# The end of a transformer block on one core: lane sums by products with ones, another order of projections, and transposes by halves

## The chip, the cores and the metric

The kernel runs on one core of one Trainium2 chip. The metric is the device time of one execution in microseconds (us); smaller is better. A core has five engines with queues of their own that run side by side and wait for one another by semaphores: TensorE (PE in the profile, PEld for its weight loads), VectorE (DVE), ScalarE (ACT), GpSimd (POOL) and SyncE (SP, which issues the DMAs here). SBUF is the memory on the core, PSUM the memory that TensorE writes its products to.

## The reference

The input x is 128 tokens of 512 features. All arithmetic is float32, apart from rounding to 8-bit floats at marked places. Three sublayers are added to x in turn:

```python
x = x + xattn(norm(x), ctx_2048, ...)   # attention to itself and to 12544 context tokens
x = x + attn(norm(x), ...)              # 16 heads of 32, causal
x = x + ffn(norm(x), ...)               # 32 experts, 8 chosen for each token
```

The first projects the tokens to 16 heads of 128 (8 groups of keys and values), attends once to the 128 tokens and once to the context, joins both results to 4096 features, divides by a scale per feature, rounds to 8-bit floats and projects back to 512. The attention to the context is `softmax(q k^T / sqrt(128)) v` with keys and values that are themselves products of the context with a weight. The second sublayer is a plain attention:

```python
Q, K, V = Xn @ Wq + bq, Xn @ Wk + bk, Xn @ Wv + bv
scores = where(causal, Q K^T / sqrt(32), -inf)
return (softmax(scores) V) @ Wo + bo
```

The third normalises, chooses 8 of 32 experts by a softmax over 32 logits, and sums `(silu(x w1) * (x v1)) w2` of the chosen ones with their weights; the kernel computes all experts and multiplies those not chosen by zero.

## The kernel before

Work is written in the order of the code, and a scheduling layer puts it into the queues of the engines; where the code says `tc.issue_after(end)`, an instruction is kept behind `end` in that order. Pools of tiles with a given number of buffers decide what must wait for what: a tile that takes over a buffer waits until the last reader of its former tile is done.

**Preamble** (lines 409 to 622): projections of the tokens, the attention of the tokens to themselves and its part of the projection back. Its first step is `norm_rows` (line 169), which normalises the rows of a 128x512 tile: statistics on VectorE (L173, L174), the variance plus epsilon on GpSimd (L179 or L181), the power -0.5 on GpSimd (L183), and the result on VectorE (L184).

**The chunk loop** (lines 798 to 825) goes over 25 chunks of the context, 512 tokens each but for one of 256. Per chunk it makes keys and values by a seven-product scheme (L329, L348), scores per group transposed, tokens on partitions (L647), a running maximum, the exponential (L729), sums over tokens (GpSimd, L739, into `ol[g][:, 1, :]`, one partial sum per partition, "lane") and the products with the values (L747, added into `ol[g][:, 0, :]` at L752). `ol[g]` is scaled on GpSimd when the maximum grows (L731).

**The end of the attention to the context** (lines 863 to 920). The last chunk's outputs of groups 0 to 7 are made in order. Between them stand the lane sums and the end of the softmax:

- `lane_sums(g, ...)` (line 757) adds the 128 lanes of a group: for each of its two heads a product with the 128 tokens' partial sums as the stationary operand and one column of ones as the moving one (L767), so that the sum of a token lands on the token's partition. For groups 6 and 7 two tiles of exponentials that GpSimd hasn't added yet are further terms. After each second group a reciprocal of 128x4 (L772) goes to `rlat`.
- `finished(b)` (line 775), for block b of two groups: four transposes of a column of `rlat`, broadcast to 128 columns, spread the reciprocals along the free dimension of every partition in PSUM (L781), and VectorE multiplies the outputs by them and by the reciprocal scale (L786).
- `round_block(b)` calls `rounded` (line 198), which rounds to 8-bit floats in six VectorE instructions: two at L203, then L209, L211, L213 and L214, whose result is `cq`.
- `proj(b, cq)` (L857): four products of 128x512 that add to `psx`. It then lets SyncE load the next weight.
- `spin` (line 873): n products of 240 columns that nobody reads, which keep TensorE at work; each stands behind the instruction given.

A float32 product is two instructions in the profile, each with a weight load.

**The second sublayer** (lines 948 to 1064). The mask is put into the scores' PSUM tile as a product with the identity (L956). `norm_rows` and four transposes into one PSUM tile (`transposed`, line 218, L222) give x^T, whose four parts VectorE scales (L966). Then come the queries (`project_T`, 16 products at L978, bias on ScalarE at L984), the values (four products of 512 at L991, bias on VectorE at L996), the keys (`project_T`), the scores of 16 heads (L1007, 16 products of 32 rows) and four fillers. For each of four sets of four heads: maximum (L1022), subtraction (L1024), exponential (L1027), four transposes, copy (L1033), and products with the values (L1036), whose last column is the sum of the softmax. Division (L1044, L1045), transposes, two copies (ScalarE L1053, VectorE L1054), the product with Wo (L1059), seven fillers, and x2 (L1064). PSUM tile `rest_ps` holds half of the products with the values; its unread end takes the fillers.

**The third sublayer** (lines 1068 to 1146): `norm_rows`, four transposes, two copies (L1076, L1077), logits (L1080), the choice of experts (L1082 to L1100), and 16 pairs of experts, `up` (L1111) and `down` (L1132). SyncE loads the first four pairs while the second sublayer runs (L942, L943, L946); the weights of the second sublayer are loaded through the same queue (L135), in the order of the list at line 838.

## Time and profile before

| | |
|---|---|
| median of three runs | 2197.46 us (2194.74 to 2199.66) |
| the profiled execution | 2197.58 us |
| its span, first to last instruction | 2195.8 us |
| mean granted TensorE clock | 0.995 |
| TensorE busy | 2158.6 us (98%) |
| VectorE, ScalarE, GpSimd busy | 1298.3, 900.3, 1075.0 us |
| last lane sums of the last chunk to x1 (L767 first, L958) | 1987.86 to 2020.48 us |
| second sublayer, x1 to x2 (end of L958 to end of L1064) | 2020.48 to 2053.61 us |
| third sublayer, to the store of the result (L1146) | 2053.65 to 2192.65 us |

The page of a profile lists the busy time of each engine, the chain of waits that ended last, and groups of instructions by source line. The timeline lists instructions of one engine, merged when equal ones follow each other: start, length, engine, line, output and inputs, how many, and in brackets how long the engine had sat idle and what released it. An engine that is busy all the time needn't be at full speed: the granted clock (PEclk, 1.00 is full) is a column of its own in the answers by stages. `xN` counts instructions, so a float32 product counts twice.

### The profile page before, as it was taken

How to read it: one execution, taken by the hardware profiler on the slowest of the kernel's cores; microseconds unless marked ns; L12 is line 12 of the kernel's file. 1: busy time of each engine (PE TensorE's matmuls, PEld its weight loads, DVE VectorE, ACT ScalarE, POOL GpSimd, SP SyncE). 2: the span in 40 equal slices, each digit the busy share in tenths (PEclk: the TensorE clock that was granted, in tenths of full speed). 3: DMA queues.
4: the chain of work that ended last, by engine and by line, in shares of the span. 5: the costliest groups of instructions: out<-in, count | busy, mean ns of one | idle time of the engine just before them, and what ended most of it. 6: DMA issues, size and time to landing. Idle time of an engine off the chain costs nothing.

```text
span 2195.8 us, 23886 instructions
## 1 busy us (share of the span) xinstructions
PE 2158.6 (98%) x8700; PEld 1539.2 (70%) x8700; DVE 1298.3 (59%) x2410; ACT 900.3 (41%) x1686; POOL 1075.0 (49%) x1165
## 2 busy tenths in 40 slices
PE   7999999999999999999899999999999999999999
PEld 3667767766776777677667776776777677676654
DVE  7565764675566457557675576567556646757311
ACT  2443444454345444434354344345434444541211
POOL 2314644764564466457554574475457447534000
PEclk9999999999999999999999999999999999999999
DMA  8300000000000000000000000000000000007593
GB/s 296 124 26 1 20 20 1 20 20 0 20 20 20 1 20 20 0 10 20 20 20 0 20 20 20 1 19 20 1 20 19 20 1 20 0 1 264 192 284 118
DMA packets 71221, 95.48 MB, mean 43 GB/s; under 512 B 3136, under 2 KB 39488, under 8 KB 71104
## 3 DMA queue, kind: packets, MB, share of 16 engines
q1 hardware_dynamic: 71104, 93.97, 13.0%
q8 instruction: 68, 1.11, 0.2%
q14 instruction: 49, 0.40, 0.1%
HBM read 93.69 MB, written 0.26 MB: 43 GB/s over the span
## 4 chain that ended last, share of the span: by engine, by line
PE 91%; DVE 5%; POOL 2%; ACT 1%; issue 1%; SPq 0%; DMA 0%; POOLq 0%; ACTq 0%; DVEq 0%
PE a_ps L329 15%; PE o_ps L747 15%; PE s_ps L647 14%; PE a_ps L348 14%; PE c_ps L329 7%; PE c_ps L348 7%; PE gu_ps L1111 4%; PE b_ps L348 4%; PE b_ps L329 4%; PE moe_acc L1132 2%; PE ps_p L462 1%; PE ps_proj L857 1%; PE ps_core L612 1%; POOL ol L739 1%; DVE mxr L658 1%
## 5 line engine op out<-in xcount | busy, mean ns | idle before, releaser
L739 POOL TENSOR_TENSOR ol<-ol,s 128x256 f32<-128x256 f32 x764 | 553.1, 732 | 31.2
L652 ACT ACTIVATE s<-s_ps,krs 128x256 f32<-128x256 f32 x784 | 324.0, 471 | 190.5 <-PE s_ps L647 178.4
L384 POOL TENSOR_TENSOR krs<-kve,mhalf 128x16 f32<-128x16 f32 (+1 forms) x50 | 142.9, 2859 | 528.4 <-DVE kve L382 528.4
L731 POOL TENSOR_TENSOR ol<-ol,al 128x512 f32<-128x512 f32 x192 | 243.5, 1280 | 295.0 <-DVE al L708 295.0
L647 PE MATMUL s_ps<-qxT,KT 128*128 128x256 f32 x1568 | 373.2, 381 | 2.8 <-ACT s L652 2.1
L747 PE MATMUL o_ps<-s,V 128*128 128x256 f32 x1568 | 371.0, 379 | 0.3 <-DVE V L318 0.3
L647 PEld LDWEIGHTS s_ps<-qxT,KT 128*128 128x128 f32 x1568 | 295.6, 190 | 104.6 <-issue 68.2
L658 DVE TRANSPOSE_TENSOR_REDUCE mxr<-s 128x32 f32<-128x1024 f32 (+1 forms) x200 | 242.9, 1215 | 188.0 <-ACT s L652 185.0
L747 PEld LDWEIGHTS o_ps<-s,V 128*128 128x128 f32 x1568 | 297.0, 190 | 41.4 <-DVE V L318 1.1
L729 ACT ACTIVATE s<-s 128x1024 f32<-128x1024 f32 (+1 forms) x200 | 208.3, 1042 | 157.0 <-DVE s L725 153.4
L725 DVE TENSOR_TENSOR s<-s,b_ps 128x1024 f32<-128x1024 f32 (+1 forms) x200 | 231.5, 1169 | 0.0
L299 ACT COPY u<-a_ps 128x512 f32<-128x512 f32 (+1 forms) x198 | 114.3, 577 | 241.2 <-PE a_ps L329 196.1
L329 PE MATMUL a_ps<-ctx,wkv 128*128 128x256 f32 (+1 forms) x800 | 186.2, 375 | 0.6 <-POOL ol L731 0.6
L348 PE MATMUL a_ps<-wkv,ctx 128*128 128x512 f32 x392 | 186.2, 597 | 0.0
L752 DVE TENSOR_TENSOR ol<-ol,o_ps 128x256 f32<-128x256 f32 x192 | 80.0, 417 | 175.6 <-PE o_ps L747 164.7
L329 PEld LDWEIGHTS a_ps<-ctx,wkv 128*128 128x128 f32 x800 | 149.9, 190 | 31.0 <-issue 11.9
L365 DVE TRANSPOSE_TENSOR_REDUCE sqr<-sq 128x16 f32<-128x512 f32 (+1 forms) x200 | 128.1, 678 | 59.8 <-ACT sq L363 59.8
L363 ACT ACTIVATE sq<-KT 128x1024 f32<-128x1024 f32 (+1 forms) x100 | 104.1, 1041 | 137.0 <-DVE KT L318 93.1
L318 DVE TENSOR_TENSOR KT<-c_ps,u 128x512 f32<-128x512 f32 (+1 forms) x50 | 34.1, 681 | 146.4 <-PE c_ps L329 146.3
L348 PEld LDWEIGHTS a_ps<-wkv,ctx 128*128 128x128 f32 x392 | 74.9, 191 | 52.8 <-issue 47.3
L329 PE MATMUL a_ps<-mix,wkv 128*128 128x256 f32 (+1 forms) x400 | 98.8, 391 | 10.6 <-ACT u L299 7.1
L329 PE MATMUL c_ps<-ctx,wsum 128*128 128x256 f32 (+1 forms) x400 | 93.7, 377 | 0.0
(217 smaller groups left out, 2773.8 us busy)
## 6 DMA issues: line engine op xcount, KB each, us to landing
ctx<-in_ctxT SPq DMA_DIRECT2D x23, 1024.0 KB, 5.0
gu<-in_w SPq DMA_DIRECT2D x32, 384.0 KB, 4.7
gu<-in_v SPq DMA_DIRECT2D x32, 384.0 KB, 5.4
dn<-in_w SPq DMA_DIRECT2D x16, 768.0 KB, 4.6
w<-in_wprojT SPq DMA_DIRECT2D x8, 1024.0 KB, 5.6
w<-in_wqxT SPq DMA_DIRECT2D x4, 1024.0 KB, 9.6
w<-in_wqT SPq DMA_DIRECT2D x4, 1024.0 KB, 4.9
wkv<-in_wkvT SPq DMA_DIRECT2D x8, 256.0 KB, 7.3
```

Of the source, the lines that this page charges most:

```text
L329: nc.tensor.matmul(ps[:, j * h : (j + 1) * h], lhsT=w[:, k, (2 * u + j) * D : (2 * u + j + 1) * D], rhs=x[:, k, :], start=first and j == k ...
L348: last_mm[0] = nc.tensor.matmul(ps, lhsT=x[:, k, v * P : (v + 1) * P], rhs=w[:, k, H : 2 * H], start=first and k == 0, stop=k == 1, skip_g ...
L365: nc.vector.tensor_reduce(r[:, 2 * j + i, : n // 32], sq[:, i, :n].rearrange("p (b i) -> p b i", i=32), AX.X, ALU.add, apply_transpose=True,)
L384: nc.gpsimd.tensor_tensor(rs[:, :, :nt], ve[:, :, :nt], mhalf.rearrange("p (g t) -> p g t", g=4)[:, :, :nt], ALU.pow,)
L647: end = nc.tensor.matmul(ps[:, t - t0, :], lhsT=KT[:, g, t * P : (t + 1) * P], rhs=qxT[:, 2 * g : 2 * g + 2, :], start=True, stop=True,)
L652: nc.scalar.activation(s[:, t, :], ps[:, t - t0, :], AF.Copy, scale=rs[:, t : t + 1])
L658: nc.vector.tensor_reduce(mxr[g // 4][:, g % 4, :nt, :].rearrange("p t k -> p (t k)"), s[:, :nt, :].rearrange("p t (k i) -> p (t k) i", i=32),
L725: nc.vector.tensor_tensor(s[:, :nt, :], s[:, :nt, :], ps[:, a, None, :].to_broadcast([P, nt, HS]), ALU.subtract,)
L729: nc.scalar.activation(s[:, :nt, :], s[:, :nt, :], AF.Exp, scale=scale)
L731: nc.gpsimd.tensor_tensor(ol[g], ol[g], alb[:, a, None, :].to_broadcast([P, 2, HS]), ALU.mult)
L739: summed[0] = nc.gpsimd.tensor_tensor(ol[g][:, 1, :], first, s[:, t, :], ALU.add).ins
L747: end = nc.tensor.matmul(ps, lhsT=V[:, t, g * D : (g + 1) * D], rhs=s[:, t, :], start=t == 0, stop=t == nt - 1,)
```

## The change

Five edits, all but the first behind the chunk loop's last chunk:

1. `norm_rows`: the variance plus epsilon (L179, L181) moves from GpSimd to VectorE. The function is used three times: in the preamble and at the start of the second and third sublayers.
2. Lane sums: ones (128x128) become the stationary operand and the partial sums (128x256) the moving one, so that each sum lands on all 128 partitions at once. The transposes of `finished` go away; instead VectorE takes the reciprocal of a 128x512 PSUM tile into an SBUF tile `inv`, and L786 reads `inv`. The five fillers between the blocks go away, and `finished` and `round_block` are no longer kept behind products.
3. Order of the second sublayer: queries, keys, half of the values' products, scores, the other half; the fillers behind the scores go away, and Wk is loaded ahead of Wv. The bias of the values goes behind the first subtraction.
4. Fillers: two instead of one after the first transposes of the exponentials, none after the transposes of `av`.
5. Transposes by halves: where x^T (both sublayers) and `av`^T are made, two PSUM tiles take two transposes each (`transposed_halves`).

In the changed build the instructions of the chunk loop and of the experts' loop stand in the same order on every engine. In SyncE's queue the load of Wo stands one place earlier, ahead of the first half of the first expert.

```diff
-            nc.gpsimd.tensor_scalar(v, mv[:, 1:2], 1.0 + EPS, EPS * EPS, ALU.mult, ALU.add)
+            nc.vector.tensor_scalar(v, mv[:, 1:2], 1.0 + EPS, EPS * EPS, ALU.mult, ALU.add)
...
-            nc.gpsimd.tensor_scalar(v, mv[:, 1:2], EPS, None, ALU.add)
+            nc.vector.tensor_scalar(v, mv[:, 1:2], EPS, None, ALU.add)
...
+    def transposed_halves(tiles, src):
+
+        for i, ps in enumerate(tiles):
+            for k in range(2):
+                j = 2 * i + k
+                turned[0] = nc.tensor.transpose(
+                    ps[:, k, :], src[:, j * P : (j + 1) * P], ident
+                ).ins
+        return tiles
...
     def lane_sums(g, last):
...
-            terms = [ol[g][:, 1, x]] + [t[:, x] for t in last]
-            for t, y in enumerate(terms):
-                end = nc.tensor.matmul(
-                    ps[:, i : i + 1], lhsT=y, rhs=ones[:, 0:1], start=t == 0,
...
-        if g % 2:
-            nc.vector.reciprocal(rlat[:, 2 * g - 2 : 2 * g + 2], ps[:, g % 4 * 2 - 2 : g % 4 * 2 + 2])
-        return end.ins
...
+        if g % 2 == 0:
+            lsum[g // 2] = ps_t.tile([P, 2, HS], F32, tag="t", name="l_ps")
+        terms = [ol[g][:, 1, :]] + last
+        for t, y in enumerate(terms):
+            end = nc.tensor.matmul(
+                lsum[g // 2][:, g % 2, :], lhsT=ones, rhs=y, start=t == 0,
+                stop=t == len(terms) - 1,
             )
         return end.ins
+
+    def finished(b):
+
+        r0 = _COLS["smooth"][0] + 16 + 4 * b
+        inv = tmp.tile([P, 2, HS], F32, tag="al", name="inv", bufs=3)
+        nc.vector.reciprocal(inv, lsum[b])
+        for h in range(4):
+            x = slice((h % 2) * S, (h % 2 + 1) * S)
+            o = ol[2 * b + h // 2][:, 0, x]
+            nc.vector.scalar_tensor_tensor(
+                o, o, rcol[:, r0 + h : r0 + h + 1], inv[:, h // 2, x], ALU.mult, ALU.mult
+            )
...
-        stream += [w.rearrange("(k p) o -> p k o", p=P) for w in (aWq, aWv, aWk, aWo)]
+        stream += [w.rearrange("(k p) o -> p k o", p=P) for w in (aWq, aWk, aWv, aWo)]
...
-            end = spin(spare[:, :240], sums_of(5), 4)
+            end = sums_of(5)
+        finished(2)
+        cqs[2] = round_block(2)
         with tc.issue_after(end):
             end = proj(0, cqs[0]).ins
         with tc.issue_after(end):
-            finished(2)
-            cqs[2] = round_block(2)
             sums_of(6)
-            end = spin(spare[:, :240], sums_of(7), 1)
-        with tc.issue_after(end):
-            end = finished(3)
-            cqs[3] = round_block(3)
+            end = sums_of(7)
+        finished(3)
+        cqs[3] = round_block(3)
...
+            qa, end = project_T("bq", lambda j: bqs[:, j : j + 1], 1.0 / math.sqrt(AD))
+            ka, end = project_T("bk", lambda j: col("bk", j), 1.0, end)
...
+            with tc.issue_after(end):
+                end = v_part(range(2))
+            with tc.issue_after(end):
+                for j in range(4):
+                    for a in range(4):
+                        r = slice(a * AD, (a + 1) * AD)
+                        end = nc.tensor.matmul(
+                            sps[:, a, j, :], lhsT=qa[r, j, :], rhs=ka[r, j, :], start=False,
+                            stop=True, skip_group_check=True,
+                        ).ins
+            with tc.issue_after(end):
+                end = v_part(range(2, NK))
...
-            end = spin(unread, end, 4)
...
+                if a == 0:
+                    with tc.issue_after(sub.ins):
+                        nc.vector.tensor_tensor(
+                            va[:, :, :AD], ps_v.rearrange("s (h d) -> s h d", d=AD),
+                            bvo[:, 0, :].rearrange("s (h d) -> s h d", d=AD), ALU.add,
+                        )
...
-                if a in (0, 3):
-                    end = spin(unread, turned[0], 1)
+                end = spin(unread, turned[0], 2 if a == 0 else 1 if a == 3 else 0)
...
-                pt = transposed(pps, av.rearrange("s h d -> s (h d)"))
-            end = spin(unread, turned[0], 1)
+                transposed_halves(pts, av.rearrange("s h d -> s (h d)"))
+            end = turned[0]
             avT = post1.tile([P, 4, S], F32, name="avT")
-            nc.scalar.copy(avT[:, 0:2, :], pt[:, 0:2, :])
-            nc.vector.tensor_copy(avT[:, 2:4, :], pt[:, 2:4, :])
+            nc.scalar.copy(avT[:, 0:2, :], pts[0])
+            nc.vector.tensor_copy(avT[:, 2:4, :], pts[1])
```

More of the change, by code (lines that the diff above doesn't have):

```diff
@@ L627, in block_kernel @@
     ol = [olp.tile([P, 2, HS], F32, name=f"ol{g}") for g in range(G)]
-    rlat = keep.tile([S, NH], F32, name="rlat")
     sp = late.enter_context(tc.tile_pool(name="sp", bufs=8, side="right", reuse_waits="tile"))
@@ L757, in lane_sums @@
     def lane_sums(g, last):
-        if g % 4 == 0:
-            lsum[g // 4] = ps_t.tile([S, 8], F32, tag="t", name="l_ps")
-        ps = lsum[g // 4]
-        for h in range(2):
-            i = g % 4 * 2 + h
-            x = slice(h * S, (h + 1) * S)
-            terms = [ol[g][:, 1, x]] + [t[:, x] for t in last]
-            for t, y in enumerate(terms):
-                end = nc.tensor.matmul(
-                    ps[:, i : i + 1], lhsT=y, rhs=ones[:, 0:1], start=t == 0,
-                    stop=t == len(terms) - 1,
-                )
-        if g % 2:
-            nc.vector.reciprocal(rlat[:, 2 * g - 2 : 2 * g + 2], ps[:, g % 4 * 2 - 2 : g % 4 * 2 + 2])
+        if g % 2 == 0:
[6 more added lines that the diff above has]
+            )
         return end.ins
     def finished(b):
-        ps = ps_so.tile([P, 4, S], F32, tag="s", name="ps_inv")
         r0 = _COLS["smooth"][0] + 16 + 4 * b
+        inv = tmp.tile([P, 2, HS], F32, tag="al", name="inv", bufs=3)
+        nc.vector.reciprocal(inv, lsum[b])
         for h in range(4):
-            end = nc.tensor.transpose(
-                ps[:, h, :], rlat[:, 4 * b + h : 4 * b + h + 1].to_broadcast([S, P]), ident
-            )
-        for h in range(4):
-            o = ol[2 * b + h // 2][:, 0, (h % 2) * S : (h % 2 + 1) * S]
-            nc.vector.scalar_tensor_tensor(
-                o, o, rcol[:, r0 + h : r0 + h + 1], ps[:, h, :], ALU.mult, ALU.mult
-            )
-        return end.ins
+            x = slice((h % 2) * S, (h % 2 + 1) * S)
+            o = ol[2 * b + h // 2][:, 0, x]
+            nc.vector.scalar_tensor_tensor(
+                o, o, rcol[:, r0 + h : r0 + h + 1], inv[:, h // 2, x], ALU.mult, ALU.mult
+            )
     def maxima(c, i):
@@ L869, in sums_of @@
             )
-        spare = pps.tile([P, H], F32, tag="ps", name="spare")
         def spin(ps, after, n):
@@ L892, in block_kernel @@
             sums_of(1)
+        finished(0)
+        cqs[0] = round_block(0)
         outputs(c, 4)
@@ L895, in block_kernel @@
         with tc.issue_after(end):
-            finished(0)
-            cqs[0] = round_block(0)
             sums_of(2)
             end = sums_of(3)
+        finished(1)
+        cqs[1] = round_block(1)
         with tc.issue_after(end):
@@ L903, in block_kernel @@
         with tc.issue_after(end):
-            finished(1)
-            cqs[1] = round_block(1)
             sums_of(4)
-            end = spin(spare[:, :240], sums_of(5), 4)
+            end = sums_of(5)
+        finished(2)
+        cqs[2] = round_block(2)
         with tc.issue_after(end):
@@ L953, in block_kernel @@
             sps = pss.tile([S, 4, 4, S], F32, name="sps")
+            rest_ps = pss.tile([S, H], F32, name="ps_av2")
+            unread = rest_ps[:, H - 240 :]
             with tc.issue_after(end):
@@ L962, in block_kernel @@
             norm_rows(xnn, x1, twice=True)
-            pt = transposed(pps, xnn)
+            pts = [pps.tile([P, 2, S], F32, tag="ps", name="ps_t"), rest_ps[:, : 2 * S]]
+            pts[1] = pts[1].rearrange("p (k s) -> p k s", k=2)
+            transposed_halves(pts, xnn)
             xT = post1.tile([P, NK, S], F32, name="xT1")
@@ L966, in block_kernel @@
                 end = nc.vector.tensor_scalar(
-                    xT[:, k, :], pt[:, k, :], col("g", k), col("b", k), ALU.mult, ALU.add
+                    xT[:, k, :], pts[k // 2][:, k % 2, :], col("g", k), col("b", k),
+                    ALU.mult, ALU.add,
                 )
@@ L971, in block_kernel, with project_T @@
                 nc.vector.tensor_tensor(x1b, x1, bvo[:, 1, :], ALU.add)
-            def project_T(nm, bias, by):
+            def project_T(nm, bias, by, after=None):
                 w = next_w()
                 ps = pps.tile([P, NK, S], F32, tag="ps", name="ps_qk")
-                for j in range(NK):
-                    for k in range(NK):
-                        nc.tensor.matmul(
-                            ps[:, j, :], lhsT=w[:, k, j * P : (j + 1) * P], rhs=xT[:, k, :],
-                            start=k == 0, stop=k == NK - 1,
-                        )
+                with tc.issue_after(after) if after else nullcontext():
+                    for j in range(NK):
+                        for k in range(NK):
+                            end = nc.tensor.matmul(
+                                ps[:, j, :], lhsT=w[:, k, j * P : (j + 1) * P], rhs=xT[:, k, :],
+                                start=k == 0, stop=k == NK - 1,
+                            )
                 t = post1.tile([P, NK, S], F32, name=f"T_{nm}")
@@ L984, in project_T, with v_part @@
                     nc.scalar.activation(t[:, j, :], ps[:, j, :], AF.Identity, bias=bias(j), scale=by)
-                return t
-            qa = project_T("bq", lambda j: bqs[:, j : j + 1], 1.0 / math.sqrt(AD))
+                return t, end.ins
+            qa, end = project_T("bq", lambda j: bqs[:, j : j + 1], 1.0 / math.sqrt(AD))
+            ka, end = project_T("bk", lambda j: col("bk", j), 1.0, end)
             w = next_w()
-            ps = pps.tile([S, H], F32, tag="ps", name="ps_v")
-            for k in range(NK):
-                nc.tensor.matmul(ps, lhsT=xT[:, k, :], rhs=w[:, k, :], start=k == 0, stop=k == NK - 1)
+            ps_v = pps.tile([S, H], F32, tag="ps", name="ps_v")
+            def v_part(ks):
+                for k in ks:
+                    end = nc.tensor.matmul(
+                        ps_v, lhsT=xT[:, k, :], rhs=w[:, k, :], start=k == 0, stop=k == NK - 1
+                    )
+                return end.ins
+            with tc.issue_after(end):
[4 more added lines that the diff above has]
+                        r = slice(a * AD, (a + 1) * AD)
+                        end = nc.tensor.matmul(
+                            sps[:, a, j, :], lhsT=qa[r, j, :], rhs=ka[r, j, :], start=False,
[3 more added lines that the diff above has]
+                end = v_part(range(2, NK))
             va = post1.tile([S, AH, AD + 1], F32, name="va")
@@ L995, in block_kernel @@
                 nc.gpsimd.memset(va[:, :, AD:], 1.0)
-            nc.vector.tensor_tensor(
-                va[:, :, :AD], ps.rearrange("s (h d) -> s h d", d=AD),
-                bvo[:, 0, :].rearrange("s (h d) -> s h d", d=AD), ALU.add,
-            )
-            ka = project_T("bk", lambda j: col("bk", j), 1.0)
-            for j in range(4):
-                for a in range(4):
-                    r = slice(a * AD, (a + 1) * AD)
-                    end = nc.tensor.matmul(
-                        sps[:, a, j, :], lhsT=qa[r, j, :], rhs=ka[r, j, :], start=False, stop=True,
-                        skip_group_check=True,
-                    ).ins
             n = AH // 2 * (AD + 1)
-            rest_ps = pss.tile([S, H], F32, name="ps_av2")
             pav = [
@@ L1016, in block_kernel @@
             ]
-            unread = rest_ps[:, H - 240 :]
-            end = spin(unread, end, 4)
             for a in range(4):
@@ L1023, in block_kernel @@
                 pe = post.tile([S, 4, S], F32, tag="pe", name="pe1")
-                nc.vector.tensor_tensor(
+                sub = nc.vector.tensor_tensor(
                     pe, sps[:, a], mx[:, :, None].to_broadcast([S, 4, S]), ALU.subtract
@@ L1027, in block_kernel @@
                 nc.scalar.activation(pe, pe, AF.Exp)
+                if a == 0:
[3 more added lines that the diff above has]
+                            bvo[:, 0, :].rearrange("s (h d) -> s h d", d=AD), ALU.add,
+                        )
                 with tc.issue_after(end):
                     pt = transposed(pps, pe.rearrange("p j t -> p (j t)"))
-                if a in (0, 3):
-                    end = spin(unread, turned[0], 1)
+                end = spin(unread, turned[0], 2 if a == 0 else 1 if a == 3 else 0)
                 peT = post.tile([S, 4, S], F32, tag="peT", name="peT1")
@@ L1048, in block_kernel @@
                 )
+            pts = [pps.tile([P, 2, S], F32, tag="ps", name="ps_t") for _ in range(2)]
             with tc.issue_after(end):
-                pt = transposed(pps, av.rearrange("s h d -> s (h d)"))
-            end = spin(unread, turned[0], 1)
+                transposed_halves(pts, av.rearrange("s h d -> s (h d)"))
+            end = turned[0]
             avT = post1.tile([P, 4, S], F32, name="avT")
-            nc.scalar.copy(avT[:, 0:2, :], pt[:, 0:2, :])
-            nc.vector.tensor_copy(avT[:, 2:4, :], pt[:, 2:4, :])
+            nc.scalar.copy(avT[:, 0:2, :], pts[0])
+            nc.vector.tensor_copy(avT[:, 2:4, :], pts[1])
             w = next_w()
@@ L1072, in block_kernel @@
             norm_rows(xn, x2)
+            pts = [mps.tile([P, 2, S], F32, tag="ps", name="ps_t") for _ in range(2)]
             with tc.issue_after(end):
-                pt = transposed(mps, xn)
+                transposed_halves(pts, xn)
             xT = post1.tile([P, NK, S], F32, name="xT2")
-            nc.vector.tensor_copy(xT[:, 0:2, :], pt[:, 0:2, :])
-            nc.scalar.copy(xT[:, 2:4, :], pt[:, 2:4, :])
+            nc.vector.tensor_copy(xT[:, 0:2, :], pts[0])
+            nc.scalar.copy(xT[:, 2:4, :], pts[1])
             pl = gps.tile([S, E], F32, tag="gu", name="ps_l")
```

## The prediction

> **What bounds the kernel now.** I read the page first: it gives the span and says which engine the end follows. The profiled execution took 2197.58 us, 1.78 us of it outside its span; the median of the three runs is 2197.46 (2194.74 to 2199.66), so the profiled execution is a typical one and I add to its time.

> ```profile
> span 2195.8 us, 23886 instructions
> PE 91%; DVE 5%; POOL 2%; ACT 1%; issue 1%; SPq 0%; DMA 0%; POOLq 0%; ACTq 0%; DVEq 0%
> ```

> TensorE sets the time almost everywhere. The order of instructions on each engine in the changed build shows the chunk loop and the experts' loop untouched, so only the stretch from about 1987 us (last chunk) to 2058 us (first expert) matters. The chain of waits, in order of time, says what ends last there:

> ```profile
> 2000.25 3.50 PE ps_proj L857 x8
> 2004.19 2.66 PE l_ps L767 x24
> 2008.71 11.00 PE ps_proj L857 x24
> ```

> TensorE is on the chain through the projection, but the timeline of VectorE shows how near it runs behind. The last block's rounding ends at 2013.79. The 24 instructions of L857 step by 0.43 us (weight loads 0.24 idle + 0.19), so the last block of eight began at about 2016.1: VectorE has 2.3 us to spare, no more.

> ```profile
> 1992.07 0.17 DVE L772 RECIPROCAL rlat<-l_ps 128x4 f32<-128x4 f32 x1
> 1992.99 1.12 DVE L786 SCALAR_TENSOR_TENSOR ol<-ol,rcol,ps_inv 128x128 f32<-128x128 f32 x4
> 1993.44 1.27 POOL L731 TENSOR_TENSOR ol<-ol,al 128x512 f32<-128x512 f32 x1
> 1994.03 1.56 DVE L203 TENSOR_SCALAR qz_y<-ol 128x256 bf16<-128x256 f32 x2
> 1995.62 1.24 DVE L209 TENSOR_SCALAR qz_e<-qz_y 128x512 uint16<-128x512 uint16 x1
> ...
> 2013.10 0.69 DVE L214 TENSOR_TENSOR cq<-qz_z,qz_m 128x512 f32<-128x512 f32 x1
> ```

> Beside GpSimd's sums L203 and L209 take 1.56 and 1.24; alone (after 2001) they take 0.49 and 0.29. The clock, in stages of 2 us (PEclk is third from the right), shows one more cost:

> ```profile
> 2004.00:2006.00 2.00, 2.00 (x21) 2.00 (x19) 1.69 (x7) 0.00 (x0) 0.00 (x0) 1.00 0.49 80
> 2006.00:2008.00 2.00, 2.00 (x11) 1.77 (x12) 0.79 (x3) 0.00 (x0) 0.00 (x0) 0.63 1.05 400
> 2008.00:2010.00 2.00, 2.00 (x6) 1.18 (x5) 1.25 (x4) 0.00 (x0) 0.00 (x0) 0.51 0.74 240
> ```

> After the one-column products the clock is halved for some 3.4 us, though TensorE is "busy" throughout. The L857 chain lost about 0.7 us to it: 24 steps of 0.43 make 10.3, and it took 11.0.

> **The lane sums.** A product of one column costs two instructions bound by the weight load: L767 x8 in 0.95, so 0.48 us per group. One of 256 columns costs as much as L747 does, 16 instructions in 3.70: 0.46 per group. Nothing is gained or lost there. Removed are 16 transposes (L781, four times about 0.45) and five fillers (L877, about 2.1), with 4 us of TensorE. That was the path only while TensorE was the later engine.

> Added are four reciprocals of 128x512 on VectorE in place of four of 128x4 (0.17 each). No row has that shape. Smaller ones do:

> ```profile
> L116 DVE RECIPROCAL rcol<-colt x1: 235/235/235, 4.0 to 4.0; 128x16 f32<-128x16 f32 x1
> L118 DVE RECIPROCAL rcol<-colt x1: 294/294/294, 4.2 to 4.2; 128x32 f32<-128x32 f32 x1
> L1099 DVE RECIPROCAL rw<-ws x1: 165/165/165, 2060.8 to 2060.8; 128x1 f32<-128x1 f32 x1
> ```

> From 1 to 32 elements the slope is 129 ns / 31 = 4.16 ns per element, four times that of an addition (L752, 256 elements, 0.41; L1064, 512, 0.69: 1.1 ns). So one takes 0.165 + 511 x 0.00416 = 2.29 us; with the flattest pair (3.7) 2.05, with the steepest (4 to 16 elements, 4.75) 2.6. [...]

> VectorE's chain then, each step start to start from the rows of this stage: 4 reciprocals x 2.21, 16 L786 x 0.27, 8 L203 x 0.26, 4 L209 x 0.30, 4 L211 x 0.43, 4 L213 and 4 L214 x 0.70, 4 additions L752 x 0.33: 8.8 + 4.3 + 2.1 + 1.2 + 1.7 + 5.6 + 1.3 = 25.1 us from 1992.07, so 2017.1 without contention.

> Contention: L786 read its second operand from PSUM and ran at its usual pace beside GpSimd (four in 1.12). Now it reads SBUF twice. By that row it would go on freely: L203 and L209 then lose about 1.5 us in all. [...] I take 3.0, since L213, which has two SBUF inputs, took 1.10 there against 0.69 alone; the bounds are 1.2 and 3.5.

> The last block is ready at 2020.1, its products start at 2020.2 against 2016.1: **+4.1 us** (1.3 to 5.8 with the ends of both). TensorE from 1992.3 has only 21.7 us of work up to there, so it waits: the first block comes at 2004.5, six or seven idle microseconds after the sums of groups 4 and 5, and behind that wait stand proj(0), the sums of 6 and 7, and all after. A halved clock then stretches proj(0) by up to 2 us; the last reciprocal needs those sums by 2012.8, and 2004.5 + 3.43 + 2 + 2.76 = 2012.7 just meets it. I take 0, at most 1.

> **Keys ahead of values, scores between halves.** Before, the key projection follows four value products (3.43), ScalarE's bias comes bare, and the scores end at 2037.0:

> ```profile
> 2035.33 1.14 ACT L984 ACTIVATE T_bk<-ps_qk,colt 128x128 f32<-128x128 f32 x4 [5.86 <-PE ps_qk L978]
> 2037.10 0.69 DVE L1022 TENSOR_REDUCE mx<-sps 128x4 f32<-128x512 f32 x1 [4.65 <-PE sps L1007]
> 2049.18 3.70 PE L1059 MATMUL ps_wo<-w,avT 128*128 128x512 f32 x8
> ```

> Now half the value products (1.72) lie behind the scores, where fillers stood, and the other half covers ScalarE (0.5): with the transposes below the first maximum comes 2.35 us sooner. Of this about 0.6 goes back: the bias of the values (L996, 0.69) now stands in VectorE's queue ahead of the second subtraction, and the third exponential in ScalarE's behind the second copy, so the last products with the values come 1.8 us sooner.

> **Transposes by halves, and the variance on VectorE.** Normalised rows: VectorE starts after two transposes of four, -0.24 twice. Before L1059 the two copies of avT ran one behind the other; separate PSUM tiles and one filler less let the product start 0.7 sooner: 1.8 + 0.7 = 2.5 at L1059. The POOL addition (0.19, 0.25) becomes a VectorE one (0.15) with one handover less: -0.1 (in the 2.5) and -0.15. The third use, at the start, is covered by the wait for a weight at 21.6 us: 0. Sum of this stage: **-2.9 us** (-2.0 to -3.5).

> SP: the load of Wo now stands ahead of the first expert's in SP's queue and waits for proj(1), so the experts' loads start some 3 us later. They ended at 2042, the first is used at 2057.9: covered; without that cover each microsecond late is one on the end.

> **Sum and rivals.** 2197.58 + 4.1 - 2.9 = **2198.8 us**. 0.2% is 4.4 us, about what a measurement of this kernel can tell: 2193.1 to 2201.9 is "no change".

> *Main case, 70%*: VectorE takes the path over and attention gives most of it back: 2196 to 2203, 0.61 of the 0.70 within 0.2%.

> *L786 not held up, 10%*: contention 1.5 instead of 3.0: 2197.3.

> *Slower, 13%*: the reciprocal costs more per element when long. Place: the four in front of the roundings; price: four times what one takes above 2.29, whole, as VectorE has no slack left. [...] The slope of the rows speaks against it.

> *Faster, 7%*: the reciprocal runs at an addition's pace (0.69). VectorE then ends at about 2013.7 and TensorE bounds again: lane sums and proj(0) end at 2007.2, three blocks later it is 2017.5 against 2019.5. -2.0 - 2.9 gives 2192.7. The 294 ns for 32 elements speak against it (an addition of 32: 0.19).

> Beyond these, the stretch with few fillers in attention (5.4 us between two, before 4.9) may halve the clock there: up to 1.7 us, in the range. So faster 0.07, same 0.61 + 0.10 = 0.71, slower 0.09 + 0.13 = 0.22. Range 2194.5 to 2203: it leaves out most of the slower case and of the faster one, 2 in 10.

> **What would show it.** Right: rows of the new reciprocal near 2.3 us; a VectorE without gaps from 1992 to 2020; TensorE waiting for cq before proj(0); L786 above 0.3 us while GpSimd works; maxima of the scores 2.3 us sooner after x1 than now (17.4 us, 2019.73 to 2037.10). Wrong: a reciprocal of another size (each 0.1 us is 0.4 on the end), or scores that wait for something that I do not see.

## The result, and the profile after

The changed kernel took 2202.91 us in the median of 20 runs, the one before 2198.45 in 20 runs beside them: ratio 1.0021 (95% interval 1.0013 to 1.0029), 3 to 6 us slower. A second series of the changed kernel on another occasion (15 runs, 2200.13) gave 1.0011 (1.0003 to 1.0019). So it is slower, by some 2 to 5 us. The forecast was 2198.8 and "no change". The range (2194.5 to 2203) held the time, at its upper edge; "no change" did not hold, since both intervals lie above 1.

The profiled execution took 2200.46 us. First the page's span and its shares of the chain:

```profile
span 2198.7 us, 23774 instructions
PE 89%; DVE 6%; issue 2%; POOL 2%; ACT 1%; DMA 0%; SPq 0%; POOLq 0%; ACTq 0%; DVEq 0%
```

TensorE lost two points of the chain, VectorE gained one. The chain in order of time (start, length, engine, tile, line) shows where; line numbers are those of the changed kernel:

```profile
1989.29 3.27 DVE inv L782
1992.85 3.30 DVE ol L786 x4
...
2012.30 3.27 DVE inv L782
...
2017.03 8.85 PE ps_proj L856 x16
```

VectorE carries the end from 1989 to 2017, as forecast. Its timeline has the lengths (start, length):

```profile
1989.22 3.34 DVE L782 RECIPROCAL inv<-l_ps 128x512 f32<-128x512 f32 x1
1992.77 3.38 DVE L786 SCALAR_TENSOR_TENSOR ol<-ol,rcol,inv 128x128 f32<-128x128 f32 x4
1996.07 1.53 DVE L203 TENSOR_SCALAR qz_y<-ol 128x256 bf16<-128x256 f32 x2
...
2019.79 0.69 DVE L214 TENSOR_TENSOR cq<-qz_z,qz_m 128x512 f32<-128x512 f32 x1
...
2040.60 0.69 DVE L1027 TENSOR_REDUCE mx<-sps 128x4 f32<-128x512 f32 x1 [9.09 <-PE sps L1009]
```

A reciprocal takes 3.34 us, not 2.29. Four L786 take 3.38 beside GpSimd, where they took 1.12. The last block is ready at 2020.48. TensorE's timeline (in brackets its idle time and what ended it):

```profile
2003.57 5.34 PE L856 MATMUL ps_proj<-w,cq 128*128 128x512 f32 x8 [7.75 <-DVE cq L214]
...
2017.03 8.83 PE L856 MATMUL ps_proj<-w,cq 128*128 128x512 f32 x16 [2.09 <-DVE cq L214]
```

It waits 7.75 us for the first block and 2.09 for the third. Eight instructions of L856 take 3.60 alone; here the first eight take 5.34 and the last sixteen 8.83 instead of 7.20. In stages of 2 us (length of the stage, busy time of PE, PEld, DVE, ACT, POOL, then the granted clock):

```profile
2004.00:2006.00 2.00, 2.00 (x3) 0.74 (x3) 2.00 (x8) 0.00 (x0) 0.00 (x0) 0.50 0.00 0
...
2016.00:2018.00 2.00, 0.97 (x2) 0.46 (x3) 2.00 (x8) 0.00 (x0) 0.00 (x0) 0.79 0.86 253
2018.00:2020.00 2.00, 2.00 (x4) 0.97 (x3) 1.79 (x5) 0.00 (x0) 0.00 (x0) 0.50 1.00 344
```

The clock is halved twice: around 2000 to 2007, under cover of VectorE, and from 2017.1 to 2020.6, on the path. In these traces such a half-clock window lasts 3.4 us, or a multiple, at a granted clock of 0.50, and each 3.4 us take 1.7 us of work.

I compare kernels by the four stages between five points: the start of the addition of the last outputs ahead of the first reciprocal, x1 (L956, L958 before), the first maximum of the scores, x2 (L1075, L1064 before), and the end of the span. Each value is a difference of starts in VectorE's timeline of one profiled execution; the kernels are named by the experiments below.

| kernel | median us | ratio to before (95%) | to x1 | to first maximum | to x2 | to the end |
|---|---|---|---|---|---|---|
| before | 2198.45 | 1 | 27.99 | 17.37 | 15.82 | 142.88 |
| changed | 2202.91 | 1.0021 (1.0013, 1.0029) | 37.01 | 14.70 | 15.51 | 142.59 |
| changed, again | 2200.13 | 1.0011 (1.0003, 1.0019) | 34.82 | 14.70 | 19.59 | 142.55 |
| old sums | 2195.99 | 0.9989 (0.9981, 0.9997) | - | - | - | - |
| new sums only | 2207.42 | 1.0039 (1.0027, 1.0051) | 34.83 | 17.36 | 15.83 | 142.90 |
| copy | 2198.54 | 1.0000 (0.9992, 1.0008) | 28.71 | 14.71 | 18.36 | 142.61 |
| reciprocals in PSUM | 2204.03 | 1.0027 (1.0017, 1.0038) | 34.34 | 14.71 | 19.60 | 142.59 |
| fillers in the waits | 2203.93 | 1.0031 (1.0019, 1.0043) | 36.74 | 14.71 | 20.03 | 142.60 |
| wide sums | 2193.18 | 0.9980 (0.9970, 0.9989) | 26.34 | 14.71 | 20.03 | 142.53 |
| old sums, fillers | 2195.01 | 0.9990 (0.9983, 0.9997) | 27.99 | 14.71 | 15.90 | 142.56 |
| wide sums, fillers | 2192.42 | 0.9978 (0.9968, 0.9988) | 26.34 | 14.70 | 15.90 | 142.51 |
| PSUM, fillers | 2201.76 | 1.0023 (1.0014, 1.0031) | 34.36 | 14.70 | 15.90 | 142.60 |
| changed, fillers | 2201.37 | 1.0020 (1.0013, 1.0026) | 34.84 | 14.70 | 15.90 | 142.54 |

Each ratio is to runs of the kernel before that were made beside it. The same code takes the same time in each trace, to 0.1 us, but for half-clock windows on the path: 15.51 or 19.59 from the first maximum to x2 in the changed kernel, and 34.82 or 37.01 to x1 (there 1.6 of the 2.2 us are the window, the rest is VectorE beside GpSimd: L203 1.01 or 1.53). With no such window on the changed kernel's path the change costs 34.82 - 27.99 = 6.83 up to x1 and gives back 2.67 + 0.31 + 0.29 = 3.27 behind it: +3.6 us, between the two measured series. Before's 27.99 does hold a window, worth 1.65 us (see the wide sums); with none in either kernel it would be about +5.2. What lies ahead of the first point is not in the table: 1991.74 and 1992.18 us in the two traces with the old `norm_rows`, 1988.89 to 1992.24 in the eleven with the new one, windows and all. So what the first edit is worth in the preamble cannot be read here.

### The profile page after: what moved, and what is told of

Its sections match the earlier page's. It is cut to its first block, busy times and chain, and to the rows that moved or that the text cites. A ratio compares the mean times of both kernels' runs of the same rounds, so it can differ in the third digit from the quotient of the medians.

```text
span 2198.7 us, 23774 instructions
## 1 busy us (share of the span) xinstructions
PE 2151.8 (98%) x8642; PEld 1535.9 (70%) x8642; DVE 1311.0 (60%) x2413; ACT 898.9 (41%) x1686; POOL 1071.7 (49%) x1162
## 4 chain that ended last, share of the span: by engine, by line
PE 89%; DVE 6%; issue 2%; POOL 2%; ACT 1%; DMA 0%; SPq 0%; POOLq 0%; ACTq 0%; DVEq 0%
PE a_ps L339 15%; PE s_ps L656 14%; PE o_ps L756 14%; PE a_ps L358 14%; PE c_ps L339 7%; PE c_ps L358 7%; PE gu_ps L1123 4%; PE b_ps L358 4%; PE b_ps L339 4%; PE moe_acc L1144 2%; PE ps_p L472 1%; PE ps_core L622 1%; DVE inv L782 1%; POOL ol L748 1%; DVE s L734 1%
## 5 line engine op out<-in xcount | busy, mean ns | idle before, releaser
L339 PE MATMUL b_ps<-ctx,wkv 128*128 128x256 f32 (+1 forms) x400 | 93.2, 375 | 0.0
```

What stands on the lines that cost most here:

```text
L339: nc.tensor.matmul(ps[:, j * h : (j + 1) * h], lhsT=w[:, k, (2 * u + j) * D : (2 * u + j + 1) * D], rhs=x[:, k, :], start=first and j == k ...
```

## The experiments

**Which part loses.** Two kernels with one part each. *Old sums*: the changed kernel with the lane sums, fillers and order of before.

```diff
-            lsum[g // 2] = ps_t.tile([P, 2, HS], F32, tag="t", name="l_ps")
+            lsum[g // 4] = ps_t.tile([S, 8], F32, tag="t", name="l_ps")
...
-        nc.vector.reciprocal(inv, lsum[b])
+        if g % 2:
+            nc.vector.reciprocal(rlat[:, 2 * g - 2 : 2 * g + 2], ps[:, g % 4 * 2 - 2 : g % 4 * 2 + 2])
```

> The changed kernel with the lane sums, their fillers and the block order of the kernel before; everything else changed. Theory (the loss is the end of the attention to the context alone): the other edits keep their gain, 3.3 us below the kernel before (some 2195.2 where before is 2198.5), and about 8 below the changed kernel. Rival (the fillers taken out of the second sublayer, or its new order, cost part of the loss): within 1 us of the kernel before or above it.

Measured: ratio 0.9989 (0.9981 to 0.9997), some 2.4 us faster than before. The profiled execution of this kernel took 5866.7 us for a reason that was not found; its trace is not used. *New sums only*: before with the reverse of this diff, that is with the new lane sums, reciprocals and block order alone.

> The kernel before with the new lane sums, reciprocals and block order only. Theory: +9.0 us on the kernel before (some 2207.5), with four reciprocals of 3.3 us, and the first maximum of the scores 17.4 us after x1 as before. Rival (the loss is shared with the second sublayer): +4 to +5 us.

Measured: ratio 1.0039 (1.0027 to 1.0051, five runs), +8.6 us. VectorE's timeline of this kernel:

```profile
1992.52 3.34 DVE L772 RECIPROCAL inv<-l_ps 128x512 f32<-128x512 f32 x1
...
1996.06 3.40 DVE L776 SCALAR_TENSOR_TENSOR ol<-ol,rcol,inv 128x128 f32<-128x128 f32 x4
```

Up to x1 it takes 34.83 us, with no window on the path. So the lane sums lose 7 to 9 us and the rest of the change gains 2 to 3. Within the noise the two add up (8.6 - 2.4 = 6.2 against 4.6 and 2.4 measured, each uncertain by about 2).

**The reciprocal as such.** *Copy*: a copy in its place. The division by the sums of the softmax is left out here.

```diff
-        nc.vector.reciprocal(inv, lsum[b])
+        nc.vector.tensor_copy(inv, lsum[b])
```

> The changed kernel with a copy of the 128x512 sums in place of their reciprocal; the division by the softmax's sums of the attention to the context is left out (the outputs are multiplied by the sums instead). Theory (the length of the reciprocal decides): a copy steps by 0.6 us instead of 3.3, VectorE ends its chain 10 us sooner and TensorE bounds again, some 5 us below the kernel before (2193.5), 9 to 10 below the changed kernel. Rival (the halved clock and the missing fillers cost the time): at most 3 us below the changed kernel.

Measured: 2198.54, ratio 1.000: 4.4 us less than the changed kernel, about half of what was expected. VectorE's and TensorE's timelines of this kernel, one fence each:

```profile
1990.54 0.68 DVE L782 COPY inv<-l_ps 128x512 f32<-128x512 f32 x1
...
1991.47 3.89 DVE L786 SCALAR_TENSOR_TENSOR ol<-ol,rcol,inv 128x128 f32<-128x128 f32 x4
```

```profile
2000.60 5.40 PE L856 MATMUL ps_proj<-w,cq 128*128 128x512 f32 x8 [4.54 <-DVE cq L214]
...
2047.48 4.47 PE L1070 MATMUL ps_wo<-w,avT 128*128 128x512 f32 x8
```

Up to x1 it needs 28.71 us, 6.1 to 8.3 less than the changed kernel: the gain is there. In this trace 2.85 us of it are gone again between the first maximum and x2 (18.36 against 15.51), where the clock is halved between 2042 and 2050. It also shows that L786, which now takes 3.89 us instead of 1.12, keeps the first block back until 2000.6: even at a copy's pace this stage was not faster than before's 27.99 (each of the two has one window on its path). So the rival "Faster" (2192.7), too, was out of reach.

*The ruler*: nine reciprocals more, written behind the last block, which nothing reads (one run).

```diff
+        for n in (64, 128, 256, 512):
+            nc.vector.reciprocal(junk[:, :n], sums[:, :n])
+        for n in (64, 128, 256, 512):
+            nc.vector.reciprocal(junk[:, :n], held[:, :n])
+        nc.vector.reciprocal(junk[:, :P], ones)
```

> The changed kernel with nine more reciprocals behind the rounding of the last block, whose results nothing reads: of 64, 128, 256 and 512 elements from PSUM, the same from SBUF, and of 128 ones from SBUF. Theory A (a fixed price for each element, 6.2 ns beyond a start of about 0.16 us): 0.55, 0.95, 1.75 and 3.34 us, from either memory and for any values. Rival B (4.2 ns an element as the rows of 1 to 32 elements showed, the rest being the wide tile in PSUM): 0.43, 0.70, 1.2, 2.3 us from SBUF, and only the PSUM ones at 6.2 ns. The time of this kernel itself says nothing: the additional work lies on the path, about 14 us of it.

VectorE's timeline:

```profile
2020.37 0.55 DVE L921 RECIPROCAL junk<-l_ps 128x64 f32<-128x64 f32 x1
...
2021.11 0.94 DVE L921 RECIPROCAL junk<-l_ps 128x128 f32<-128x128 f32 x1
...
2024.72 3.35 DVE L921 RECIPROCAL junk<-l_ps 128x512 f32<-128x512 f32 x1
...
2032.38 1.73 DVE L923 RECIPROCAL junk<-held 128x256 f32<-128x256 f32 x1
2034.14 3.35 DVE L923 RECIPROCAL junk<-held 128x512 f32<-128x512 f32 x1
2037.53 0.95 DVE L924 RECIPROCAL junk<-ones 128x128 f32<-128x128 f32 x1
```

From 64 to 512 elements the slope is (3.35 - 0.55) / 448 = 6.25 ns per element, from PSUM and SBUF and for ones alike. The short rows of before don't lie on this line: at 16 and 32 elements it gives 250 and 350 ns, and they took 235 and 294.

**The wait of L786.** *Reciprocals in PSUM*: `inv` in a PSUM tile, so that L786 reads SBUF once only.

```diff
-        inv = tmp.tile([P, 2, HS], F32, tag="al", name="inv", bufs=3)
+        inv = ps_so.tile([P, 2, HS], F32, tag="s", name="inv")
```

> The changed kernel with the reciprocals in PSUM, so that the multiplication by them has only one input in SBUF. Theory (the first four multiplications take 3.4 us because GpSimd reads SBUF then): they take 1.1 us, and the end comes 2.2 us sooner than in the changed kernel. Rival (two SBUF inputs or the wait for the reciprocal make them slow by themselves): no change, or the later twelve get faster as well.

VectorE's timeline:

```profile
1994.48 1.09 DVE L786 SCALAR_TENSOR_TENSOR ol<-ol,rcol,inv 128x128 f32<-128x128 f32 x4
```

The wait is gone: 1.09 instead of 3.38, beside the same sums on GpSimd, while the later twelve are as long as before (0.33 each). So this experiment's rival is out. The median shows nothing of it (2204.03). TensorE's timeline says where the 2.3 us go:

```profile
2016.33 8.54 PE L856 MATMUL ps_proj<-w,cq 128*128 128x512 f32 x16 [3.25 <-DVE cq L214]
```

With VectorE earlier, the fourth reciprocal runs ahead of the third block's L209 (in the changed kernel, ahead of its L213). TensorE then waits 3.25 us for that block, and a window falls on the sixteen products behind the wait (8.54 instead of 7.20). Up to x1 it took 34.34 us, only 0.5 less than the changed kernel without a window (34.82). In this trace the stage to x2 took 19.60, with windows from 2046 to 2057.

**The half clock.** Three experiments tried to drive it away. *Fillers in the waits*: 14 and 3 fillers where TensorE of the changed kernel waits.

```diff
-            end = sums_of(5)
+            end = spin(spare[:, :240], sums_of(5), 14)
...
+            if b == 1:
+                end = spin(spare[:, :240], end, 3)
```

> The changed kernel with filler products in TensorE's two waits: 14 (6.5 us) behind the lane sums of groups 4 and 5, 3 (1.4 us) behind the products of the second block. Theory A (the part of the loss that the reciprocal doesn't explain is TensorE's half clock, which follows its idle waits; in the changed kernel's trace one such window of 3.4 us lies on the path at 2017.4 and costs 1.7 us): no window between 2000 and 2021 in the trace, proj of the last two blocks in 7.2 us instead of 8.8, and 1.7 to 3 us less than the changed kernel's 2202.9, so about 2200.5. Rival B (the windows come on their own and have nothing to do with the waits): 2202.9 within 1 us and still a window in that stretch.

TensorE's timeline:

```profile
1998.99 5.83 PE L874 MATMUL spare<-qxT,ident 128*128 128x240 f32 x28
...
2020.09 8.83 PE L856 MATMUL ps_proj<-w,cq 128*128 128x512 f32 x16 [2.01 <-DVE cq L214]
```

The covered window at 2000 to 2007 is gone, the one on the last blocks is not (8.83 again), and three more lie in the attention. 2203.93: the theory missed its time. It does not speak against the waits as a cause, though: the first block now came at full clock, TensorE was done sooner, and behind the three fillers it still waited 2.01 us for the third block, where the changed kernel waited 2.09.

*Wide sums*: as old sums, with 64 columns of ones.

```diff
-                    ps[:, i : i + 1], lhsT=y, rhs=ones[:, 0:1], start=t == 0,
+                    ps[:, i, :], lhsT=y, rhs=ones[:, 0:64], start=t == 0,
```

> The changed kernel with the lane sums, fillers and order of before (as in the experiment with the old sums), but each of the sums' products against 64 columns of ones instead of one, the first column being read. Theory A (TensorE's clock is halved after stretches in which few columns are streamed, even where the engine counts as busy: before's window at 2006.5 follows 32 one-column products): no window at about 2003 to 2010, the sums' products little longer (0.12 to 0.18 us each, 2 us in all, mostly beside VectorE), and 0 to 1.7 us less than the old sums' 0.9989 of before's time: ratio 0.998 to 0.999. Rival B (the longer products lie on the path, the window stays): ratio 0.999 to 1.000.

TensorE's timeline, then the stage of 2 us that was at clock 0.63 before:

```profile
1992.03 1.00 PE L777 MATMUL l_ps<-ones,ol 128*128 128x64 f32 x8
...
2006.83 10.47 PE L867 MATMUL ps_proj<-w,cq 128*128 128x512 f32 x24
```

```profile
2006.00:2008.00 2.00, 2.00 (x10) 1.21 (x10) 1.76 (x6) 0.00 (x0) 0.00 (x0) 1.00 1.01 337
```

The eight products cost 1.00 instead of 0.95, no window follows, and x1 comes after 26.34 us instead of 27.99. Ratio 0.9980 (0.9970 to 0.9989), better than either kernel, though windows at 2040 to 2051 lay in the profiled execution.

*Fillers in the attention*: one behind the transposes of the second quarter and one between the halves of the last transposes, tried with four kernels.

```diff
-                end = spin(unread, turned[0], 2 if a == 0 else 1 if a == 3 else 0)
+                end = spin(unread, turned[0], (2, 1, 0, 1)[a])
...
-                transposed_halves(pts, av.rearrange("s h d -> s (h d)"))
+                transposed_halves(pts[:1], avf)
+            end = spin(unread, turned[0], 1)
+            with tc.issue_after(end):
+                transposed_halves(pts[1:], avf[:, 2 * P :])
```

With the old sums:

> The changed kernel with the lane sums, fillers and order of before, and two more filler products in the attention of the second sublayer: one behind the transposes of the second quarter, one between the two halves of the transposes of the context. Theory A (the changed attention, with fewer fillers, lets TensorE's clock fall there in many executions, as in the traces of the two runs whose windows lay at 2042 to 2057 and cost 3 to 4 us): mean granted clock up by 0.0005 to 0.001 and 1 to 2 us less than with the old sums alone: ratio about 0.998. Rival B (the fillers don't change the clock, each lies partly on the path): ratio 0.999 or a little over it.

With the wide sums:

> The old sums with 64 columns of ones (2193.2, ratio 0.998), and two more fillers in the attention of the second sublayer. Theory A (half-clock windows of 3.4 us in the attention, of which that kernel's trace showed three at 2040 to 2051, come from too few streamed columns there): no window between 2030 and 2060, mean clock 0.9955 or more, first maximum to x2 15.9 us instead of 20.0, ratio about 0.9970 to 0.9975. Rival B (the windows come anyway, or typical executions have none there): ratio 0.998 to 0.9985, the fillers' own 0.4 us.

With the reciprocals in PSUM:

> The changed kernel with the reciprocals written to PSUM (which took L786's wait for GpSimd away, 2.3 us, and 2.7 us from the stage up to x1, but gave no gain in the median, 2204.0, since first maximum to x2 took 19.6 us instead of 15.5 under three half-clock windows), and the two fillers in the attention. Theory A (the windows there ate the gain, and the fillers keep them away): first maximum to x2 15.9 us, 2200.0 to 2201.0 at the clock of before's runs, ratio about 1.001. Rival B (writing to PSUM costs elsewhere): ratio 1.0027 again.

With the changed kernel as it is:

> The changed kernel with the two fillers in the attention and nothing else. Theory A (part of the changed kernel's lower mean clock, 0.9931 against 0.9943, is windows in the attention of some executions): mean clock about 0.9937, 1 to 1.5 us less than the changed kernel, ratio about 1.0015. Rival B (none): 0.4 us more than the changed kernel, ratio 1.0023.

In all four traces the stage from the first maximum to x2 is 15.90 us, 0.39 more than the undisturbed 15.51, and holds no window; of the seven other traces with the changed attention (the ruler's among them) six held one or more. Over all runs the mean granted clock rose as well: 0.9936 to 0.9942, 0.9952 to 0.9955, 0.9930 to 0.9942, and 0.9931 and 0.9937 to 0.9940. The ratios hardly moved: 0.9990 against 0.9989, 0.9978 against 0.9980, 1.0023 against 1.0027, and 1.0020 between the two series of the changed kernel. Theory A is borne out in the traces and in the clock; a gain in time, of 1 to 2 us at most, is less than these ratios can tell. Wide sums with fillers are the best version run, 2192.42 us, 0.22% under before.

*The changed kernel again*, for a second trace.

> The changed kernel once more, for a second trace. Theory A (where the half-clock windows lie differs between executions of one kernel, the work between them does not): the four reciprocals at 3.34 us and the stage from the addition of the last outputs but four to x1 at 35.3 to 37.0 us by whether a window lies on the last two blocks' products, against 28.0 before; ratio 1.002. Rival B (the window at 2017 is the same in every execution): 37.0 again, with the window at the same place.

TensorE's timeline:

```profile
2005.26 5.86 PE L856 MATMUL ps_proj<-w,cq 128*128 128x512 f32 x8 [7.19 <-DVE cq L214]
...
2018.71 7.20 PE L856 MATMUL ps_proj<-w,cq 128*128 128x512 f32 x16 [1.57 <-DVE cq L214]
```

Same work, other windows: none on the last sixteen (7.20), 34.82 us up to x1, but three windows between 2047 and 2058. The place of a window is a matter of the single execution; the 3.34 us of a reciprocal are not.

**What comes ahead of a window.** The 13 traces that can be used settle this. In each of them all windows start on one grid of 3.413 us, to within 0.005 us, and the grid lies elsewhere in every execution. I divided the traces along their grids. Here are four pairs of neighbouring steps (the columns as in the stages above). Before, with the one-column products in the first step:

```profile
2003.13:2006.54 3.41, 3.41 (x30) 3.09 (x28) 2.52 (x8) 0.00 (x0) 0.00 (x0) 1.00 0.45 110
2006.54:2009.95 3.41, 3.41 (x10) 2.41 (x11) 1.99 (x7) 0.00 (x0) 0.00 (x0) 0.50 0.88 312
```

The wide sums, at the same place in the code:

```profile
2002.75:2006.16 3.41, 3.41 (x31) 3.31 (x29) 2.32 (x9) 0.00 (x0) 0.00 (x0) 1.00 0.51 166
2006.16:2009.57 3.41, 3.41 (x13) 1.80 (x12) 3.27 (x11) 0.00 (x0) 0.00 (x0) 1.00 0.78 257
```

The changed kernel, with the wait of 2.09 us in the first step, and the changed kernel again, with the wait of 1.57 us:

```profile
2013.73:2017.14 3.41, 1.32 (x4) 0.30 (x3) 3.41 (x5) 0.00 (x0) 0.00 (x0) 1.00 0.26 54
2017.14:2020.55 3.41, 3.41 (x5) 1.35 (x6) 3.13 (x9) 0.00 (x0) 0.00 (x0) 0.50 1.01 355
```

```profile
2016.47:2019.88 3.41, 1.84 (x5) 0.68 (x4) 3.38 (x9) 0.00 (x0) 0.00 (x0) 1.00 0.42 79
2019.88:2023.29 3.41, 3.41 (x9) 1.36 (x8) 2.10 (x4) 0.00 (x0) 0.00 (x0) 1.00 1.03 363
```

For each step I added up the moving columns of TensorE's instructions, at some 0.83 ns a column (512 columns step by 0.43 us; twice that at half clock), as a share of the step. In the first steps of the four pairs this share is 0.26, 0.58, 0.34 and 0.46: half clock follows the first and the third. With 64 columns instead of one TensorE is busy for the same 3.41 us, but it streams more.

Between 40 and 2190 us the 13 traces have 8176 steps. At full clock, 70 steps were followed by half clock, all with a share of 0.38 or less; 8006 were not, all with 0.37 or more. At half clock, 31 steps were followed by half clock again, with 0.72 or less, and 69 by full clock, with 0.77 or more. So in these traces what is streamed in one step goes with the clock of the next, whether a wait or narrow products thin it out, and where the grid lies decides whether a thin stretch fills a step. The fillers in the waits fit in: the step with the wait of 2.01 us had 0.33.

If the grid is moved along all its positions, the attention of the changed kernel would get a window in about four of ten, by my estimate from its trace, and with the fillers in fewer than one of ten. So it was partly chance that six of seven traces had one.

## Why the prediction was wrong, and where it was right

- **The step that failed: "So one takes 0.165 + 511 x 0.00416 = 2.29 us".** It measured 3.34 to 3.36 in every trace that has it. The slope came from rows of 1 to 32 elements, which are not long enough to show the price of an element; from 64 on it is 6.25 ns. Four times (3.34 - 2.29) is +4.2 us, the term of the sum that was mis-sized. The path it lies on was right. By the sum, "no change" ends at a reciprocal of 2.29 + (4.4 - 1.2) / 4 = 3.1 us (0.2% of the time is 4.4 us, 1.2 of it forecast), and 3.34 is above that; the price of the rival "Slower", four times what one takes above 2.29, gives 2198.8 + 4.2 = 2203.0. The rows ended at 32 elements and the new instruction has 512, so the 0.22 for the slower side was too small.
- **VectorE takes over the path: right.** No gap in its timeline from 1989 to 2020, TensorE waiting 7.75 us for the first block (forecast: six or seven).
- **VectorE's other steps: 1.6 us too long.** From the stage's start to the last `cq` the changed kernel took 31.0 us without a window; less 4 x 3.27 for reciprocals and 2.9 for contention in that trace, 15.0 remain, where 16.6 was summed (16.3 and the first addition). I had L213 and L214 at 0.70 apart; between steps of another block they are 0.54 and 0.60 apart, which is some 0.6 of the 1.6; the rest is spread over the other steps. That this partly made up for the reciprocals is luck, and it kept the time inside the range. So +4.1 became 4.1 + 4.2 - 1.6 = 6.7, measured 6.83.
- **Contention: right.** 3.0 forecast; no run shows that term as such: it was my estimate, taken between 1.2 and 3.5 because L213 took 1.10 beside GpSimd against 0.69 alone. The runs showed in its place that L786 lost 2.3 us (3.38 against 1.12), L203 0.5 to 1.0 (1.01 and 1.53 against 0.49), L209 0.1 (0.41 against 0.29). The row that spoke for free running had the second operand in PSUM; with it there the same four L786 took 1.09 beside GpSimd, with both operands in SBUF 3.38.
- **The clock: "I take 0, at most 1".** On the first block's products this held: they took 5.34 and 5.86 instead of 3.60, and the last reciprocal still had its sums in time. On the last blocks' products a window cost 1.6 us in one of two traces of the changed kernel, which is above the bound. It makes the runs differ; the +3.6 us by the stages stand without it.
- **Second sublayer: right.** -2.9 forecast, -3.27 by stages (-2.67 at the first maximum, forecast 2.35). The experts' loads stayed covered: x2 to the end is 0.3 shorter.
- **Sum.** 4.1 - 2.9 = +1.2 forecast; 6.83 - 3.27 = +3.6 by the stages; +4.6 and +2.4 by the medians.

Still open is why the trace of the old sums took 5866.7 us, and why reciprocals of 16 and 32 elements lie under the line of the long ones. For the reciprocals in PSUM both traces show the wait of 3.25 us and the window behind it, which leave 0.5 of the 2.3 us; that most executions are like these two is likely after so long a wait, but not shown.

## What to carry to other kernels

A price per element is read from a row long enough that the fixed start is small in it; a slope taken from the first 32 elements was a third too low (4.16 against 6.25 ns). Before an engine with 2.3 us of slack is given 13 us of work, work out the price at which the decision turns (here 3.1 us a reciprocal; 2.29 forecast, 3.34 measured), and if the rows stop far short of the new shape, as at 32 of 512 elements, give the other side of it more of a chance. Where one value serves 128 columns, invert it once and spread it with TensorE: 4 x 0.17 us and sixteen products against 4 x 3.34. And before a theory of the clock is tested with fillers, count what TensorE streams in each 3.4 us (here half clock set in only behind steps with 0.38 or less): fillers must close the thin stretch; to stand near it is not enough.
